# Selective-scan network in float32: B and C rows in one transfer per tile, layer 1's transfers on one queue, sums of pairs one unit later

## The chip, the cores and the metric

The kernel runs on one core of one Trainium2 chip. Its time is device microseconds of one execution, as the median of several. Everything is float32.

## The reference, cut to what matters

Four residual layers work on an image batch of 4 x 64 x 64 pixels with 192 channels, each on a group-normalised input. Layers 0 and 3 are two-dimensional selective scans (four directions over 4096 pixels), layer 1 is four Mamba blocks over the rows and columns (lines of 64 pixels, forwards and backwards), layer 2 is a Toeplitz layer. Nearly all the time goes into the selective scans:

```
def step(h, inp):                                   # over the pixels l
    u_l, dt_l, Bl, Cl = inp
    dA = exp(dt_l[..., None] * A)
    h  = dA * h + (dt_l * u_l)[..., None] * Bl[:, None, :]
    y  = sum(h * Cl[:, None, :], axis=-1)           # over 16 states
    return h, y
```

The channels are 384 in layers 0 and 1 and 192 in layer 3. B, C and dt come from a projection of u at every pixel; delta = softplus(projection of dt + bias).

## The kernel before, in words

**Units.** A job is one direction of one stretch of T = 512 pixels of one image; each of the three scan layers has 128 jobs. In a job, a unit (t, p, c) covers 64 channels (group g = 2t + c) and 4 of the 16 states (p of 4), as a tile of 128 partitions by 1024: 64 channels times two halves of the states on the partitions, two states times 512 pixels along each. A job of layers 0 and 1 has 24 units (three t of eight), one of layer 3 has 12. The order within a t is `TWO` (p, c): (0,0) (0,1) (3,0) (1,1) (1,0) (3,1) (2,0) (2,1), or `ONE`: p = 0, 3, 1, 2.

**What a unit does.** `feed` (two units ahead, AHEAD) writes b = dt * u * B into PSUM with 16 matmuls of dtuT against diagonal tiles (L374), and dA = exp(delta * A) with two activations on ScalarE (L397). `scan` runs the recurrence on VectorE into h (L407 in layer 1, two halves at L414 in layers 0 and 3, started from `carry`) and multiplies h by C on GpSimd (L418). `collect` sums the states with matmuls against `fold` into y (L443), always for two units together: pairs go onto the list `waiting` after each second unit, and one of two entries is taken in each unit that follows. For p = 3 ("direct": both groups in layers 1 and 3, c = 1 alone in layer 0) b comes from GpSimd instead: `spread` multiplies dtu2 by bc (L347), three units ahead (EARLY).

**Tiles and transfers.** B and C of a job are written from tile `xd` to DRAM (`bc_dram`, L226) and fetched back repeated over partitions: the tile `c` per p, and `bc` for p = 3 (L335). Each is filled by two transfers, one for each half of the partitions. `both` holds delta of one group, `dtu2` holds dt * u of one group, both twice over the halves. In layers 0 and 3 they are copied from SBUF (L317); in layer 1 from DRAM (`delta_dram`, `dtu_dram`, L322), with one transfer per tile, which is written

```
src = job["deltas" if name == "both" else "dtus"][key * 64 : (key + 1) * 64, :]
nc.sync.dma_start(one, src.unsqueeze(0).broadcast_to([2, 64, T]))
```

**What sets the order.** `run_jobs` writes the program unit by unit. Steps of a job (load, project, step sizes, turns, gating, outputs) stand at unit numbers relative to the job's first unit, in `when` and `steps`; what a step returns is done one unit later (`rest`). `plan` puts each fetch at the latest of: when its source is ready, LEAD = 12 units ahead of its first use, and when the tile that had its buffer was used last plus `behind`. Tiles come from pools with a number of buffers each (`bufs`); a transfer waits until its buffer is released. [...]nearly all transfers are issued by SyncE (SP), a few by ScalarE (ACT): bc_dram and delta_dram, and y in layers 0 and 3.

Layer 1's own steps are in `mamba_job`: `input_of` (convolution), `gate` (z), `gated` (u*D + y on VectorE, then times z on GpSimd) and `out`.

Of the kernel before, what the change touches and what calls it, by code (L numbers as in the profile page):

```python
# [7 lines left out]
F32 = mybir.dt.float32  # L8
# [8 lines left out]
N = 16  # L17
R = 12
E = R + 2 * N
T = 512  # L20
# [5 lines left out]
EARLY = 3  # L26
# [10 lines left out]
class Kernel:  # L37
# [66 lines left out]
    def run_jobs(self, jobs, pools):  # L104


        G = jobs[0]["DI"] // 64
        order = []
        for t in range(-(-G // 2)):
            order += [(t, *one) for one in (TWO if 2 * t + 1 < G else ONE)]  # L110
        units = [(k, *one) for k in range(len(jobs)) for one in order]
        per = len(order)
        steps = {}
        for k, job in enumerate(jobs):
            for at, step in self.prepare(job, pools) + job["steps"]:
                steps.setdefault(k * per + at, []).append(step)
        for at, load in self.plan(jobs, order, pools):
            steps.setdefault(at, []).append(load)
        start, end = min(steps), max(len(units) + 3, max(steps) + 1)
        waiting, rest = [], []  # L120
        for i in range(min(start, -EARLY), end + 4):
            if 0 <= i + AHEAD < len(units):
                k, t, p, c = units[i + AHEAD]
                self.feed(jobs[k], t, p, c, pools)
            todo = waiting[:1]
            if 0 <= i < len(units):
                k, t, p, c = units[i]
                after = self.scan(jobs[k], t, p, c, pools)
                if after is not None:
                    steps.setdefault(i + 1, []).insert(0, after)  # L130
            if 0 <= i + EARLY < len(units):
                k, t, p, c = units[i + EARLY]
                if c in jobs[k]["direct"].get(p, ()):
                    self.spread(jobs[k], t, p, c, pools)
            if 0 <= i < len(units):
                if (i + 1) % 2 == 0:
                    waiting += [(units[i][0], [one[1:] for one in units[i - 1 : i + 1]], n) for n in range(2)]


            if todo:  # L140
                k, two, n = waiting.pop(0)
                self.collect(jobs[k], two, n, pools)
                if n and two[1][1] == LAST:
                    steps.setdefault(i, []).append(lambda job=jobs[k], t=two[0][0]: job["add"](t))
            now, rest = rest + steps.pop(i, []), []
            for step in now:
                after = step()
                if after is not None:
                    rest.append(after)
        assert not rest and not steps and not waiting  # L150

    def plan(self, jobs, order, pools):


        uses, ready = {}, {}
        for k, job in enumerate(jobs):
            job["cbc"], job["bbc"], job["diag"], job["both"], job["dtu2"] = {}, {}, {}, {}, {}
            job["dtuT"] = {}
            when = {name: k * len(order) + at for name, at in job["when"].items() if isinstance(at, int)}

            near = 2 if job["carry"] is not None else 5
            dtu = when["finish"] + 3 if job["carry"] is not None else when["store"] + 5
            for j, (t, p, c) in enumerate(order):
                i, g = k * len(order) + j, 2 * t + c
                direct = c in job["direct"].get(p, ())
                reads = [("c", p, i, when["project"] + 6), ("both", g, i - AHEAD, when["finish"] + near)]
                if direct:
                    reads += [("bc", p, i - EARLY, when["project"] + 6), ("dtu2", g, i - EARLY, dtu)]
                else:
                    reads.append(("diag", p, i - AHEAD, when["turn_b"] + 5))  # L170
                for name, key, at, after in reads:
                    first, _ = uses.setdefault(name, {}).get((k, key), (at, at))
                    uses[name][k, key] = first, at
                    ready[name, k] = after
        loads = []
        for name, of in uses.items():
            bufs, turn = pools["bufs"][name], sorted(of, key=of.get)
            for j, (k, key) in enumerate(turn):
                first = of[k, key][0]
                at = max(ready[name, k], first - LEAD)  # L180
                if j >= bufs:
                    at = max(at, of[turn[j - bufs]][1] + pools["behind"])
                one = lambda part=None, job=jobs[k], name=name, key=key: self.fetch(job, name, key, pools, part)
                if name == "diag":


                    at = max(ready[name, k], first - (LEAD_DIAG if k else NB))
                    if j >= bufs:
                        at = max(at, of[turn[j - bufs]][1] + 3)
                    loads += [(first, at + part, lambda part=part, one=one: one(part)) for part in range(NB)]  # L190
                    at += NB - 1
                else:
                    loads.append((first, at, one))
                assert at < first, (name, k, key, at, first)
        return [one[1:] for one in sorted(loads, key=lambda one: one[0])]

    def prepare(self, job, pools):

        nc = self.nc
        prep, mm = pools["prep"], pools["mm"]  # L200
        P, NT, DI, w = job["P"], job["NT"], job["DI"], job["w"]
# [12 lines left out]
        def projected(ps):  # L214
            xd = job["xd"] = prep.tile([128, 256], F32, name="xd", bufs=1)
# [7 lines left out]
            else:  # L223
                by_half = job["bc"].rearrange("a (h l) -> h a l", h=2)
            for h in range(2):
                nc.scalar.dma_start(by_half[h], xd[h * 64 : h * 64 + 2 * N, :])  # L226
            job["delta"] = prep.tile([P, NT, T], F32, name="delta", bufs=1)
            job["dtu"] = prep.tile([P, NT, T], F32, name="dtu", bufs=1)
            if P < 128:
# [37 lines left out]
        def finish():  # L267
            delta = job["delta"]
            nc.scalar.activation(delta, delta, AF.Softplus)  # L269
            if job["carry"] is None:  # L270
                job["deltas"] = self.bcd.tile([DI, T], F32, name="delta_dram")
                nc.scalar.dma_start(job["deltas"].rearrange("(t p) l -> p t l", p=P), delta)

            def after():
                (nc.gpsimd if job["carry"] is None else nc.vector).tensor_mul(job["dtu"], delta, job["u"])  # L275

            return after

        def turn(t):
            ps = mm.tile([128, NB, P], F32, name="dtu_ps", tag="mm")  # L280
# [24 lines left out]
    def fetch(self, job, name, key, pools, part):  # L305
# [23 lines left out]
        else:  # L329
            one = pools[name].tile([128, 2 * T], F32, name=name)  # L330
            job["cbc" if name == "c" else "bbc"][key] = one
            for q in range(2):
                row = N + 8 * q + 2 * key if name == "c" else 4 * key + 2 * q
                src = job["bc"][row : row + 2, :].rearrange("a l -> (a l)")
                nc.sync.dma_start(one[q * 64 : (q + 1) * 64, :], src.unsqueeze(0).broadcast_to([64, 2 * T]))  # L335

    def spread(self, job, t, p, c, pools):

# [61 lines left out]
    def scan(self, job, t, p, c, pools):  # L400
# [1 line left out]
        rev, carry, g = job["rev"], job["carry"], 2 * t + c  # L402
        way = slice(None, None, -1) if rev else slice(None)
        b, dA, direct = job["fed"].pop((t, p, c))
        h = pools["work"].tile([128, 2 * T], F32, name="h", bufs=7 if carry is None else 3)
        if carry is None:
            nc.vector.tensor_tensor_scan(h[:, way], dA[:, way], b[:, way], 0.0, ALU.mult, ALU.add)  # L407
        else:
# [143 lines left out]
    def ss2d_scan(self, pre, u_d, y_d, P, NT, ways, A, dtb):  # L552
# [3 lines left out]
        with (  # L556
# [10 lines left out]
            tc.tile_pool(name="s_y", bufs=2, space=PSUM) as yp,  # L567
        ):
            pools = {"prep": prep, "work": work, "c": cp, "diag": dp, "both": both, "mm": mm, "b": bp, "y": yp,
                     "bc": bcp, "dtu2": dtu2, "bufs": bufs, "behind": 3}  # L570
            jobs = []
            carry = {
                (g, p): pw.tile([128, 2], F32, name=f"carry{g}_{p}", bufs=1)
                for g in range(DI // 64) for p in range(PAIRS)
            }
            when = {
                3: dict(load=-33, project=-29, turn_b=-27, step_size=(-21, -19, -17), finish=-15,
                        turn=(-13, -11, -9), direct={3: (1,)}),
                2: dict(load=-25, project=-21, turn_b=-19, step_size=(-17, -16), finish=-14,
                        turn=(-9, -8), direct={3: (0, 1)}),  # L580
            }[NT]
# [122 lines left out]
    def mamba(self, x_in):  # L704
# [6 lines left out]
        done = [[self.dram.tile([C, L], F32, name=f"m_out{i}_{b}") for b in range(B)] for i in range(2)]  # L711

        both_w = [self.dram.tile([P, NT, C], F32, name=f"m_both_w{i}") for i in range(4)]
        bufs = dict(c=4, bc=2, diag=4, both=4, dtu2=2)
        with (
            tc.tile_pool(name="n", bufs=2) as pn,
            tc.tile_pool(name="n_ps", bufs=2, space=PSUM) as psum,
# [27 lines left out]
        with (  # L745
# [12 lines left out]
            tc.tile_pool(name="m_y", bufs=2, space=PSUM) as yp,  # L758
        ):
            pools = {"prep": prep, "work": work, "c": cp, "diag": dp, "both": both, "mm": mm, "b": bp, "y": yp,  # L760
                     "bc": bcp, "dtu2": dtu2, "bufs": bufs, "behind": 2}
            fixed = [once.tile([P, 2 * T], F32, name=f"dA{j}") for j in range(3)]
            zero = once.tile([P, 2 * ROWS], F32, name="zero")
            nc.gpsimd.memset(zero, 0.0)
# [13 lines left out]
    def mamba_job(self, pw, pin, mm, i, begin, rev, w, x, done, both_w, c, fixed, zero):  # L778
# [69 lines left out]
        def gated(t):  # L848
# [3 lines left out]
                nc.vector.scalar_tensor_tensor(u, u, w["D"][:, t : t + 1], job["y"][t], ALU.mult, ALU.add)  # L852
                nc.gpsimd.tensor_mul(z, z, u)

            return after

        def parts(m):

# [30 lines left out]

            return after  # L890

        when = dict(project=-24, turn_b=-22, step_size=(-20, -19, -17), finish=-15, turn=(-9, -2, 3), store=-11)
        each = lambda f, ats: [(at, lambda t=t: f(t)) for t, at in enumerate(ats)]
        steps = [(-50, weights)] if begin else []
        steps += [(-46, load)] + each(input_of, (-37, -34, -31)) + each(gate, (-4, -1, 1)) + each(out, (30, 33))
        if rev:
            steps += each(earlier, (25, 28))
        job.update(
# [327 lines left out]
```

## Time and profile before

| | us |
|---|---|
| median of 3 runs | 31297.76 (31268.2 to 31301.49) |
| profiled execution | 31284.29 |
| its span | 31282.5 |
| scan of layer 0, each of four images | about 2278 (the first from 190.2 to 2468.4) |
| scan of layer 1 | 11188.7 (10806.8 to 21995.5) |
| scan of layer 3, each of four images | about 1264 to 1267 (the first from 25158.1 to 26421.8) |

The rest, some 5,700 us, is the inputs and outputs of layers 0 and 3, the norms and layer 2. The table by stretch gives, for every engine, the time in which it was busy; the share of the DMA engines is a mean over the core's 16. TensorE's busy time comes from modelled ends of matmuls, so that 90% is not its peak rate.

### The profile page before, as it was taken

How to read it: one execution, taken by the hardware profiler on the slowest of the kernel's cores; microseconds unless marked ns; L12 is line 12 of the kernel's file. 1: busy time of each engine (PE TensorE's matmuls, PEld its weight loads, DVE VectorE, ACT ScalarE, POOL GpSimd, SP SyncE). 2: the span in 40 equal slices, each digit the busy share in tenths (PEclk: the TensorE clock that was granted, in tenths of full speed). 3: DMA queues.
4: the chain of work that ended last, by engine and by line, in shares of the span. 5: the costliest groups of instructions: out<-in, count | busy, mean ns of one | idle time of the engine just before them, and what ended most of it. 6: DMA issues, size and time to landing. Idle time of an engine off the chain costs nothing. (4 is left out here: it accounts for less than half of the span.)

```text
span 31282.5 us, 503240 instructions
## 1 busy us (share of the span) xinstructions
PE 27353.4 (87%) x189464; PEld 16218.5 (52%) x189464; DVE 22344.0 (71%) x16587; ACT 23257.2 (74%) x50327; POOL 22884.2 (73%) x9831
## 2 busy tenths in 40 slices
PE   8998998998899699999889999998588988888888
PEld 5664654665466355555555555555355344444444
DVE  7887887888788677776667777676423277777777
ACT  7885885887688588887878888887232187878788
POOL 7885885888688499988889898888100077777777
PEclk9999999999999899999999999999799999999999
DMA  3333333333333433333333333333533344444444
GB/s 108 102 99 116 103 96 117 99 99 107 109 103 100 139 96 98 97 97 98 96 98 98 97 98 96 97 97 96 133 72 78 106 132 126 132 126 130 127 131 126
DMA packets 1606616, 3342.20 MB, mean 107 GB/s; under 512 B 350646, under 2 KB 407415, under 8 KB 1588567
## 3 DMA queue, kind: packets, MB, share of 16 engines
q1 hardware_dynamic: 1432150, 3033.08, 35.3%
q10 hardware_dynamic: 172032, 276.92, 2.6%
q8 instruction: 1497, 24.53, 0.3%
q14 instruction: 937, 7.67, 0.1%
HBM read 2149.81 MB, written 656.08 MB: 90 GB/s over the span
## 5 line engine op out<-in xcount | busy, mean ns | idle before, releaser
L374 PE MATMUL b<-diag,dtuT 128*64 128x256 f32 x98304 | 13308.4, 386 | 954.9 <-DVE h L414 759.4
L418 POOL TENSOR_TENSOR hc<-h,c 128x1024 f32<-128x1024 f32 x4608 | 10938.8, 2394 | 1641.9 <-DVE h L414 1336.6
L374 PEld LDWEIGHTS b<-diag,dtuT 128*64 128x64 f32 x98304 | 8544.2, 139 | 5362.7 <-issue 1770.1
L397 ACT ACTIVATE dA<-both,A 128x512 f32<-128x512 f32 (+1 forms) x12288 | 8308.5, 711 | 2062.3 <-DVE h L414 981.2
L414 DVE TENSOR_TENSOR_SCAN h<-dA,carry,b 128x512 f32<-128x512 f32 x6720 | 8180.2, 1263 | 1546.4 <-PE b L374 647.5
L418 POOL TENSOR_TENSOR h<-h,c 128x1024 f32<-128x1024 f32 x3072 | 7209.3, 2376 | 918.1 <-DVE h L407 570.0
L328 ACT ACTIVATE diag<-ident,bt 128x128 f32<-128x128 f32 x20480 | 6563.7, 391 | 106.9 <-issue 106.1
L407 DVE TENSOR_TENSOR_SCAN h<-dA,b 128x1024 f32<-128x1024 f32 x2304 | 5240.7, 2279 | 1701.4 <-PE b L374 829.2
L443 PE MATMUL y<-hc,fold 128*64 128x512 f32 x18432 | 5587.0, 605 | 534.0 <-POOL hc L418 533.3
L443 PE MATMUL y<-h,fold 128*64 128x512 f32 x12288 | 4736.9, 614 | 716.2 <-POOL h L418 713.0
L347 POOL TENSOR_TENSOR bs<-dtu,bc 128x1024 f32<-128x1024 f32 x1536 | 3642.2, 2371 | 452.8 <-issue 224.8
L497 POOL MEMSET pad<- 128x13068 f32 (+1 forms) x8 | 73.4, 9172 | 3974.3 <-DMA cw<-in_L_conv_w 3001.6
L443 PEld LDWEIGHTS y<-hc,fold 128*64 128x64 f32 x18432 | 1709.8, 139 | 1684.1 <-POOL hc L418 978.7
L397 ACT ACTIVATE b<-both,A 128x504 f32<-128x504 f32 (+1 forms) x3072 | 2074.0, 675 | 527.9 <-DVE h L414 438.3
L443 PEld LDWEIGHTS y<-h,fold 128*64 128x64 f32 x12288 | 1321.9, 139 | 1804.2 <-POOL h L418 1210.7
L407 DVE TENSOR_TENSOR_SCAN h<-b,bs 128x1024 f32<-128x1024 f32 x768 | 1752.7, 2282 | 650.8 <-ACT b L397 616.2
L414 DVE TENSOR_TENSOR_SCAN h<-b,carry,bs 128x512 f32<-128x512 f32 x1344 | 1638.8, 1260 | 111.8 <-ACT b L397 93.7
L235 PEld LDWEIGHTS dtu_ps<-ident,dtu 128*64 128x64 f32 (+1 forms) x16384 | 1165.4, 143 | 649.4 <-issue 307.6
L235 PE MATMUL dtu_ps<-ident,dtu 128*64 128x128 f32 (+1 forms) x16384 | 1309.6, 278 | 171.2 <-ACT z L839 125.3
L397 ACT ACT_TABLE_LOAD x1094 | 1403.6, 1283 | 15.2 <-DMA both<-delta_dram 2.6
L414 DVE TENSOR_TENSOR_SCAN h<-dA,b 128x512 f32<-128x512 f32 x960 | 1113.5, 1205 | 365.2 <-PE b L374 139.9
L275 DVE TENSOR_TENSOR dtu<-delta,u 128x1536 f32<-128x1536 f32 (+1 forms) x256 | 589.0, 2301 | 560.5 <-ACT delta L269 560.5
(157 smaller groups left out, 26136.2 us busy)
## 6 DMA issues: line engine op xcount, KB each, us to landing
c<-bc_dram SPq DMA_DIRECT2D x3072, 256.0 KB
both<-delta SPq DMA_DIRECT2D x2048, 128.0 KB
bc<-bc_dram SPq DMA_DIRECT2D x768, 256.0 KB
both<-delta_dram SPq DMA_DIRECT2D x768, 256.0 KB
dtu<-dtu_dram SPq DMA_DIRECT2D x768, 256.0 KB
dtu<-dtu SPq DMA_DIRECT2D x1280, 128.0 KB
L_y<-out ACTq DMA_DIRECT2D x512, 256.0 KB
u<-L_u SPq DMA_DIRECT2D x160, 768.0 KB
```

The lines of the kernel that those rows point to most:

```text
L235: nc.tensor.matmul(to[half * 64 : (half + 1) * 64], of[:, half * 64 : (half + 1) * 64], self.ident[:p, :p], start=True, stop=True,)
L275: (nc.gpsimd if job["carry"] is None else nc.vector).tensor_mul(job["dtu"], delta, job["u"])
L328: nc.scalar.activation(to, self.ident, AF.Copy, scale=of)
L347: self.nc.gpsimd.tensor_mul(by(b), dtu, by(job["bbc"][p]))
L374: nc.tensor.matmul(to, dtu, job["diag"][p][:, k, 2 * q : 2 * q + 2, :], start=True, stop=True,)
L397: nc.scalar.activation(to[n], of, AF.Exp, scale=w["A"][:, g, 2 * p + n : 2 * p + n + 1])
L407: nc.vector.tensor_tensor_scan(h[:, way], dA[:, way], b[:, way], 0.0, ALU.mult, ALU.add)
L414: nc.vector.tensor_tensor_scan(hn[:, n, way], dA[:, n, way], by_n[:, n, way], start, ALU.mult, ALU.add)
L418: nc.gpsimd.tensor_mul(hc, h, job["cbc"][p])
L443: nc.tensor.matmul(y[c * 64 : (c + 1) * 64, :], self.fold, of, start=first == 0 and n == 0, stop=last == LAST and n == 1)
L497: nc.gpsimd.memset(pad, 0.0)
```

## The change

- `fetch`: a `c` or `bc` tile is filled by one transfer for all 128 partitions, in all three scan layers; the source is a hand-written access pattern.
- `run_jobs`: in layer 1 (`lag` 1) a pair of units may be summed one unit later; in layers 0 and 3 (`lag` 0) as before.
- In layer 1 the stores to bc_dram and delta_dram are issued by SyncE; the latter stands one unit later.
- In layer 1 several steps stand at other units; `gated` returns its work one unit later; five c and three dtu2 buffers in place of four and two; `behind` is 3 in place of 2.
- In layers 0 and 3: four h buffers in place of three; in layer 0 the turns of dtu one unit later; the product dtu one unit later, with `near` and `dtu` to match.

```diff
 # run_jobs
-            todo = waiting[:1]
+            todo = waiting[:1] if waiting and waiting[0][0] <= i else []
...
                 if (i + 1) % 2 == 0:
-                    waiting += [(units[i][0], [one[1:] for one in units[i - 1 : i + 1]], n) for n in range(2)]
+                    two = [one[1:] for one in units[i - 1 : i + 1]]
+                    waiting += [(i + 1 + pools["lag"], units[i][0], two, n) for n in range(2)]
 # plan
-            near = 2 if job["carry"] is not None else 5
-            dtu = when["finish"] + 3 if job["carry"] is not None else when["store"] + 5
+            near = 3 if job["carry"] is not None else 5
+            dtu = when["finish"] + 4 if job["carry"] is not None else when["store"] + 5
 # prepare: projected
-                nc.scalar.dma_start(by_half[h], xd[h * 64 : h * 64 + 2 * N, :])
+                dma = nc.sync if job["carry"] is None else nc.scalar
+                dma.dma_start(by_half[h], xd[h * 64 : h * 64 + 2 * N, :])
 # prepare: finish
                 job["deltas"] = self.bcd.tile([DI, T], F32, name="delta_dram")
-                nc.scalar.dma_start(job["deltas"].rearrange("(t p) l -> p t l", p=P), delta)

             def after():
+                if job["carry"] is None:
+                    nc.sync.dma_start(job["deltas"].rearrange("(t p) l -> p t l", p=P), delta)
                 (nc.gpsimd if job["carry"] is None else nc.vector).tensor_mul(job["dtu"], delta, job["u"])

-            return after
+            return after if job["carry"] is None else lambda: after
 # fetch
-            for q in range(2):
-                row = N + 8 * q + 2 * key if name == "c" else 4 * key + 2 * q
-                src = job["bc"][row : row + 2, :].rearrange("a l -> (a l)")
-                nc.sync.dma_start(one[q * 64 : (q + 1) * 64, :], src.unsqueeze(0).broadcast_to([64, 2 * T]))
+            row, step = (N + 2 * key, 8) if name == "c" else (4 * key, 2)
+            of = job["bc"]
+            nc.sync.dma_start(one, bass.AP(of.tensor, of.offset + row * T, [[step * T, 2], [0, 64], [1, 2 * T]]))
 # scan
-        h = pools["work"].tile([128, 2 * T], F32, name="h", bufs=7 if carry is None else 3)
+        h = pools["work"].tile([128, 2 * T], F32, name="h", bufs=7 if carry is None else 4)
 # ss2d_scan, layer 0
-                        turn=(-13, -11, -9), direct={3: (1,)}),
+                        turn=(-12, -10, -8), direct={3: (1,)}),
 # mamba
-        bufs = dict(c=4, bc=2, diag=4, both=4, dtu2=2)
+        bufs = dict(c=5, bc=2, diag=4, both=4, dtu2=3)
...
-                     "bc": bcp, "dtu2": dtu2, "bufs": bufs, "behind": 2}
+                     "bc": bcp, "dtu2": dtu2, "bufs": bufs, "behind": 3, "lag": 1}
 # mamba_job: gated
-            return after
+            return lambda: after
 # mamba_job
-        when = dict(project=-24, turn_b=-22, step_size=(-20, -19, -17), finish=-15, turn=(-9, -2, 3), store=-11)
+        when = dict(project=-24, turn_b=-22, step_size=(-21, -19, -18), finish=-14, turn=(-9, -3, 8), store=-11)
-        steps += [(-46, load)] + each(input_of, (-37, -34, -31)) + each(gate, (-4, -1, 1)) + each(out, (30, 33))
+        steps += [(-46, load)] + each(input_of, (-36, -34, -31)) + each(gate, (-6, -4, -1)) + each(out, (33, 35))
```

More of the change, by code (lines that the diff above doesn't have):

```diff
@@ L120, in run_jobs @@
         waiting, rest = [], []
-        for i in range(min(start, -EARLY), end + 4):
+        for i in range(min(start, -EARLY), end + 6):
             if 0 <= i + AHEAD < len(units):
@@ L136, in run_jobs @@
                 if (i + 1) % 2 == 0:
-                    waiting += [(units[i][0], [one[1:] for one in units[i - 1 : i + 1]], n) for n in range(2)]
+                    two = [one[1:] for one in units[i - 1 : i + 1]]
+                    waiting += [(i + 1 + pools["lag"], units[i][0], two, n) for n in range(2)]
             if todo:
-                k, two, n = waiting.pop(0)
+                _, k, two, n = waiting.pop(0)
                 self.collect(jobs[k], two, n, pools)
@@ L569, in ss2d_scan @@
             pools = {"prep": prep, "work": work, "c": cp, "diag": dp, "both": both, "mm": mm, "b": bp, "y": yp,
-                     "bc": bcp, "dtu2": dtu2, "bufs": bufs, "behind": 3}
+                     "bc": bcp, "dtu2": dtu2, "bufs": bufs, "behind": 3, "lag": 0}
             jobs = []
```

## Prediction

> **What bounds the kernel now.** I read the page's first part, then the sums by stretch for the three scan stages, then the DMA view of short windows in which only one kind of transfer is on the wire. The page (busy us, share of the span, instructions):
>
> ```profile
> span 31282.5 us, 503240 instructions
> PE 27353.4 (87%) x189464; PEld 16218.5 (52%) x189464; DVE 22344.0 (71%) x16587; ACT 23257.2 (74%) x50327; POOL 22884.2 (73%) x9831
> ```
>
> No engine is full over the span, so the stages are read one by one: one image's scan in layer 0, all of layer 1's scan, one image's scan in layer 3 (start:end, length, busy us of PE, PEld, DVE, ACT, POOL, granted clock, DMA share, GB/s):
>
> ```profile
> 190.20:2468.40 2278.20, 2117.10 (x16610) 1370.47 (x16610) 1955.74 (x1612) 1899.48 (x4704) 2018.58 (x862) 0.97 0.37 98
> 10806.80:21995.50 11188.70, 10189.26 (x69944) 5865.09 (x69944) 7950.70 (x4715) 9341.64 (x17095) 9858.99 (x4359) 0.97 0.31 97
> 25158.10:26421.80 1263.70, 1102.30 (x8118) 661.78 (x8118) 992.56 (x828) 1172.50 (x2996) 1146.96 (x480) 0.99 0.49 131
> ```
>
> A layer-0 image is 32 jobs of 24 units: 2278.2/32 = 71.2 us a job. Layer 1 is 128 jobs of 24 units: 87.4 us. A layer-3 image is 32 jobs of 12 units: 39.5 us. TensorE (93%) and GpSimd (89%) bound layer 0, TensorE (91%) and GpSimd (88%) layer 1; in layer 3 TensorE, ScalarE and GpSimd are all near 90%. The DMA share looks harmless everywhere, 0.31 to 0.49, but it is a mean over 16 engines. Issues in all, and KB each:
>
> ```profile
> c<-bc_dram SPq DMA_DIRECT2D x3072, 256.0 KB
> bc<-bc_dram SPq DMA_DIRECT2D x768, 256.0 KB
> both<-delta_dram SPq DMA_DIRECT2D x768, 256.0 KB
> dtu<-dtu_dram SPq DMA_DIRECT2D x768, 256.0 KB
> ```
>
> Two windows take that mean apart. First, two c and two bc transfers (issued from 768.15 us on), nearly alone:
>
> ```profile
> DMA packets 320, 1.07 MB, mean 227 GB/s; under 512 B 63, under 2 KB 63, under 8 KB 319
> q1 hardware_dynamic: 319, 1.05, 89.6%
> ```
>
> 256 data packets of 4 KB in 4.7 us, all 16 engines busy, and 63 tiny packets: the four transfers' completion marks, about 16 each. Second, a window of 10.6 us in layer 1 (17917.3 to 17927.9) in which two both<-delta_dram transfers run, with SyncE's queue around it:
>
> ```profile
> DMA packets 250, 0.51 MB, mean 48 GB/s; under 512 B 2, under 2 KB 2, under 8 KB 250
> q1 hardware_dynamic: 250, 0.51, 12.6%
> 17915.32 1.16 SPq L322 DMA_DIRECT2D both<-delta_dram  x2
> 17920.93 0.48 SPq L322 DMA_DIRECT2D dtu<-dtu_dram  x1
> ```
>
> The same kind of transfer at 48 GB/s, on 12.6% of the engines: two of sixteen, with two marks. The two were issued within 1.2 us and run one after the other, **5.3 us each**: they share the same two engines, first come first served. So layer 1 already has a narrow place: both and dtu are 768/128 = 6 each a job, 12 x 5.3 = 63.6 of 87.4 us on two engines.
>
> [...]the source of both<-delta_dram is [2 copies][64 rows][512], [...]two marks; a c transfer is [64][1024], about 16 marks.[...]
>
> **The change part by part.**
>
> *B and C in one transfer (all three layers).* Removed: two transfers of [64][1024]. Added: one whose source is [2, step][64, step 0][1024] and whose target is 128 partitions. The outermost source size is 2, the form of both<-delta_dram, with packets of 4 KB in place of 2 KB. Price: twice 5.3 = **10.6 us on the two engines** (64 packets each), in place of two transfers at 4.7/4 = 1.2 us on sixteen. Bounds: 10.2 if a longer packet carries less overhead; 2.4 if the pattern is spread after all. Per job 4 c and 1 bc, 3072/2/384 and 768/2/384: 5 x 10.6 = 53.0 us. SyncE issues five transfers fewer a job (0.58 us each), which pays nothing, since it mostly waits.
>
> - Layer 1: 63.6 + 53.0 = 116.6 us a job on two engines. They also carry 1/16 of the rest: two 768 KB stores, 384 KB of xn, 384 KB out, half as often 384 KB in, some 160 KB per engine at 24 GB/s = 6.5 us. SyncE waits for the delta and dtu stores to land before it issues the next both, with little queued behind: about 3 us idle (it waited 78.2/64 = 1.2 us for one such store). Sum **126 us** against 87.4: +38.6 x 128 = **+4,940**. Ends: 118 (marks hidden, lower packet price) to 140 (idle gaps as below).
> - Layer 3: 53.0 + 6.5 (some 2.5 MB a job of both, dtu, u, out over 16) + 1.5 for gaps = **61 us** against 39.5: +21.5 x 128 = **+2,750**. Ends 55 and 68.
> - Layer 0: 53.0 + 11 (4.2 MB over 16) = 64 us, under 71.2, so no throughput limit, but a burst. Three c tiles can only be loaded once the last tasks of the job before have released theirs (units 17, 20, 21), and the last is read at unit 27: 10 units, 30 us. Before, they took 7 us; now 3 x 10.6 = 31.8 plus small transfers and landing, 33.5. GpSimd waits some 4 us, and the two bounding engines can make up part of it; I take **+4 us x 128 = +510**. Ends 0 (caught up) and +1,000.
>
> *Pairs summed a unit later (layer 1).* No instruction added; the y matmuls move one unit (3.6 us) back, past waits of TensorE for GpSimd: 1210.7 us (705 times) on weight loads and 713.0 us (485) on matmuls. What is late next is the gating of u by y. At best layer 1 falls to GpSimd's 9859 us, a gain of 1,330; at worst it costs some us a job where u is needed. Behind a queue of 126 us a job GpSimd has 40 us to spare, so I take **0**; the cover is the narrow pair of engines, and without it I would take half, -500 or so, with what follows.
>
> *All transfers by SyncE (layer 1).* Two bc_dram stores and one delta store a job leave ScalarE's queue, with ScalarE's wait for bc_dram (337.4 us, 54 times). On SyncE they stand in order between the loads: behind them queue the dtu, bc and both loads, and if ScalarE is late with delta all wait. Between -337 and +3 us a job; the gain is hidden like the last, the loss is in my 3 us of gaps.
>
> *Steps respaced, five c and three dtu2 buffers.* Instructions unchanged; loads start earlier. It smooths a queue but cannot add to the rate of two engines: 0, from -200 to +200.
>
> *Four h buffers, later dtu turns (layers 0 and 3).* VectorE waited 28.0 us an image for GpSimd in layer 0: at most -110 over four images. In layer 3 it is covered by the transfers. 0 is taken.
>
> Sum: 31,284 (the profiled execution, 31282.5 plus 1.8 around it; the shown median is 13 above, under 0.05%) + 4,940 + 2,750 + 510 = 39,484, about **39,480 us**.
>
> **The rivals.** *Spread over 16 engines (faster).* If the step of 4096 or 1024 in place of 0 in the outer dimension lets the transfer use 16 engines, nothing gets narrower and the waits above count: half of GpSimd's 1,330 idle us in layer 1, less some new lateness, about -550: 30,730 us. Against it: the order of sizes is that of both<-delta_dram, which ran on two. It decides from the first c transfer: 16 marks or 2. Chance 0.05, of which 0.01 within the noise.
>
> *Only layer 1 pays (slower, less).* Loads are asked for up to 12 units ahead, so layers 0 and 3 may hide them: 31,284 + 4,940 = 36,220. Against it: 53 us a job cannot hide under 39.5 in layer 3, whatever the lead. Chance 0.04.
>
> *The queue also stands idle (slower, more).* SyncE issues in order and waits for releases: 978.3 and 1527.7 us in layer 1 for GpSimd before line 322. If each wait now leaves the pair idle, with c tiles freed late and needed soon, layer 1 goes to 140, layer 3 to 68, layer 0 to +8 us: 31,284 + 6,730 + 3,650 + 1,020 = 42,700. For it: three c loads in one burst. Against: with compute ahead of its data the releases come early. Chance 0.16; the forecast keeps 0.75.
>
> **The numbers.** Lower ends together (118, 55, 0) give 37,190, upper ones 42,700; the range 36,900 to 42,300 leaves out the first two rivals and the worst of the third. Differences under 0.2% (63 us) count as none. Faster 0.04, same 0.01, slower 0.95.
>
> **What would show it.** Right: c transfers of 512 KB with two marks each at about 48 GB/s; GpSimd's scan products waiting for "DMA c<-bc_dram" (298.1 us over the whole run now) by thousands of us; all engines' shares down in layers 1 and 3, layer 0 nearly as before; layer 1's scan near 16.1 ms, layer 3's near 1.95 ms an image. Wrong: c transfers at over 200 GB/s, or layer 3 still at 39.5 us a job.

## The result, and the profile after

The changed kernel takes 40700.38 us (median of 4 runs, 40699.81 to 40713.34) against 31299.62 us for the kernel before beside it: a ratio of 1.3006, interval 1.2983 to 1.3028. That is 1,220 us above the forecast of 39,480 and inside its range. From the page of the profiled execution:

```profile
span 40697.9 us, 499183 instructions
PE 28508.9 (70%) x189464; PEld 16515.4 (41%) x189464; DVE 22385.6 (55%) x16587; ACT 23005.2 (57%) x50179; POOL 22906.4 (56%) x9831
DMA c<-bc_dram 16%; DMA both<-delta_dram 15%; PE b L376 8%; ACT diag L331 5%; ACT dA L399 5%; PE y L445 4%; DVE h L416 3%; POOL hc L420 2%; ACT L399 2%; ACT b L399 2%; DVE h L409 2%; SPq L325 2%; PE yt_ps L1078 1%; DMA xn<-t_xn 1%; PE conv_ps L531 1%
c<-bc_dram SPq DMA_DIRECT2D x1536, 512.0 KB
bc<-bc_dram SPq DMA_DIRECT2D x384, 512.0 KB
```

VectorE and GpSimd do what they did, to 50 us; their shares fall because the span grew. The third line is the chain that ended last, by line: transfers lead it, and its first two entries are the ones on a pair of engines: 12.6% of sixteen for both<-delta_dram in the prediction's second window, 13.1% for c in the view below. Half as many c and bc issues carry the same bytes. By stretch (columns as before): one image of layer 0, layer 1, one image of layer 3.

```profile
208.10:2869.00 2660.90, 2253.43 (x16610) 1573.71 (x16610) 1960.48 (x1612) 1899.24 (x4704) 2021.38 (x863) 0.91 0.28 84
12460.80:28239.30 15778.50, 10583.67 (x69942) 5309.36 (x69942) 7959.29 (x4715) 9104.49 (x16956) 9871.16 (x4359) 0.85 0.19 69
31431.50:33452.30 2020.80, 1148.32 (x8118) 672.11 (x8118) 996.89 (x828) 1168.72 (x2996) 1144.16 (x478) 0.81 0.26 82
```

Per job: layer 1 went from 87.4 to 123.3 us, layer 3 (mean of four images) from 39.5 to 63.5, layer 0 from 71.1 to 83.2. The mean DMA share fell in every stage, to 0.19 in layer 1, exactly where transfers became the bound: a mean over 16 engines does not see two. The DMA view of 17.4 us in layer 3 (32473.2 to 32490.6), in which c transfers are nearly alone, and SyncE's queue around it:

```profile
DMA packets 228, 0.91 MB, mean 52 GB/s; under 512 B 2, under 2 KB 2, under 8 KB 228
q1 hardware_dynamic: 228, 0.91, 13.1%
32449.24 0.54 SPq L337 DMA_DIRECT2D bc<-bc_dram  x1
32457.08 21.24 SPq L337 DMA_DIRECT2D c<-bc_dram  x4
32478.37 15.79 SPq L320 DMA_DIRECT2D both<-delta  x6
```

Two marks, 13.1% of sixteen engines, 52 GB/s: 226 packets of 4 KB on two engines in 17.4 us, 154 ns a packet and 9.9 us a tile. Marks are the packets under 512 B: in the prediction's second window two of them came between 17922 and 17923 us and two between 17927.5 and 17928.5, at the end of each transfer. The last two lines show something more. The column after the start runs from the beginning of a row's first issue to the end of its last, with waits for a free tile between them. The single issues follow (ns, shortest/median/longest): those two rows, then c in the layer-3 image after and before.

```profile
L337 SPq DMA_DIRECT2D c<-bc_dram x4: 482/1403/9789, 32457.1 to 32468.5; - x4
L320 SPq DMA_DIRECT2D both<-delta x6: 507/596/11509, 32478.4 to 32493.7; - x6
L337 SPq DMA_DIRECT2D c<-bc_dram x124: 482/551/12116, 31441.7 to 33415.3; - x124
L335 SPq DMA_DIRECT2D c<-bc_dram x248: 444/584/829, 25179.4 to 26384.2; - x124
```

Most issues still take some 0.55 us. But with a few long transfers outstanding one issue stood for 9.8 us and the next, of a small both transfer, for 11.5 us; in the kernel before no c issue of the image took over 0.83 us.

Who waited for whom, layer 1 first (total us, times, longest), then one image of layer 0:

```profile
ACT dA L399 <- DMA both<-delta_dram: 5315.1, 375, 31.2
POOL h L420 <- DMA c<-bc_dram: 2645.1, 128, 31.7
...
POOL hc L420 <- DMA c<-bc_dram: 237.9, 25, 11.9
```

In layer 1 the both tiles, whose transfers were not touched, are the ones most waited for: they share the pair with the c tiles. An experiment below takes them off it. In layer 0 one job looks like this, SyncE's queue first and then GpSimd, with its idle time and what ended it:

```profile
1016.11 0.55 SPq L337 DMA_DIRECT2D c<-bc_dram  x1
1025.08 2.88 SPq L337 DMA_DIRECT2D c<-bc_dram  x2
1052.92 4.66 POOL L420 TENSOR_TENSOR hc<-h,c 128x1024 f32<-128x1024 f32 x2 [7.37 <-DMA c<-bc_dram]
```

Three c loads are issued as tiles come free, and the product that needs the last of them starts 36.8 us after the first, 7.4 us after GpSimd was ready for it.

### The profile page after: what moved, and what is told of

Read it like the earlier page. It is cut to its first block, busy times and chain, and to the rows that moved or that the text cites. A ratio compares the mean times of both kernels' runs of the same rounds, so it can differ in the third digit from the quotient of the medians.

```text
span 40697.9 us, 499183 instructions
## 1 busy us (share of the span) xinstructions
PE 28508.9 (70%) x189464; PEld 16515.4 (41%) x189464; DVE 22385.6 (55%) x16587; ACT 23005.2 (57%) x50179; POOL 22906.4 (56%) x9831
## 4 chain that ended last, share of the span: by engine, by line
DMA 37%; PE 22%; ACT 21%; DVE 8%; issue 5%; POOL 4%; SPq 3%; ACTq 0%; POOLq 0%; DVEq 0%
DMA c<-bc_dram 16%; DMA both<-delta_dram 15%; PE b L376 8%; ACT diag L331 5%; ACT dA L399 5%; PE y L445 4%; DVE h L416 3%; POOL hc L420 2%; ACT L399 2%; ACT b L399 2%; DVE h L409 2%; SPq L325 2%; PE yt_ps L1078 1%; DMA xn<-t_xn 1%; PE conv_ps L531 1%
## 5 line engine op out<-in xcount | busy, mean ns | idle before, releaser
L376 PE MATMUL b<-diag,dtuT 128*64 128x256 f32 x98304 | 14287.1, 408 | 3766.7 <-DVE h L409 2610.0
L376 PEld LDWEIGHTS b<-diag,dtuT 128*64 128x64 f32 x98304 | 8876.0, 147 | 8540.2 <-DVE h L409 3240.1
L445 PE MATMUL y<-hc,fold 128*64 128x512 f32 x18432 | 6476.9, 618 | 1166.3 <-POOL hc L420 1162.7
L445 PE MATMUL y<-h,fold 128*64 128x512 f32 x12288 | 3786.4, 627 | 2420.2 <-POOL h L420 2420.2
L445 PEld LDWEIGHTS y<-hc,fold 128*64 128x64 f32 x18432 | 2080.6, 142 | 2408.0 <-POOL hc L420 1628.2
L445 PEld LDWEIGHTS y<-h,fold 128*64 128x64 f32 x12288 | 1061.1, 146 | 3438.6 <-POOL h L420 2538.9
L426 ACT COPY carry<-h 128x2 f32<-128x2 f32 x4608 | 821.0, 183 | 1795.7 <-DMA dtu<-dtu 1630.6
L825 DVE SCALAR_TENSOR_TENSOR u<-in_ps,conv_w,u 128x504 f32<-128x504 f32 (+2 forms) x1152 | 832.2, 723 | 1773.5 <-ACT u L820 1764.0
L292 ACT COPY dtuT<-dtu_ps 128x512 f32<-128x512 f32 (+1 forms) x1024 | 560.5, 547 | 2066.6 <-issue 1040.9
```

The costliest lines, as they stand in the source:

```text
L376: nc.tensor.matmul(to, dtu, job["diag"][p][:, k, 2 * q : 2 * q + 2, :], start=True, stop=True,)
L426: nc.scalar.copy(carry[g, p], hn[:, :, 0 if rev else T - 1])
L445: nc.tensor.matmul(y[c * 64 : (c + 1) * 64, :], self.fold, of, start=first == 0 and n == 0, stop=last == LAST and n == 1)
L825: nc.vector.scalar_tensor_tensor(u[:, :, to], ps[:, :, of], tap(3 - j), u[:, :, to], ALU.mult, ALU.add)
```

## The experiments

Each edit is against the changed kernel if nothing else is said; each ratio is to the kernel before, measured beside it. Stage lengths run from the start of the first product with C to the start of the last.

**Two halves again**

```diff
-            row, step = (N + 2 * key, 8) if name == "c" else (4 * key, 2)
-            of = job["bc"]
-            nc.sync.dma_start(one, bass.AP(of.tensor, of.offset + row * T, [[step * T, 2], [0, 64], [1, 2 * T]]))
+            for q in range(2):
+                row = N + 8 * q + 2 * key if name == "c" else 4 * key + 2 * q
+                src = job["bc"][row : row + 2, :].rearrange("a l -> (a l)")
+                nc.sync.dma_start(one[q * 64 : (q + 1) * 64, :], src.unsqueeze(0).broadcast_to([64, 2 * T]))
```

> The changed kernel with one part undone: each c or bc tile is filled by two transfers of 64 partitions again; everything else of the change stays. Theory (narrow pair: the whole loss comes from the merged transfer's outermost size of 2, which puts it on two DMA engines): the loss is gone and the waits taken out of layer 1 count, about 30,800 us (30,300 to 31,300), layer 1's scan 10,600 to 11,150 us. Rival (order: stores to bc_dram and delta_dram among the loads on SyncE, or the later sums, carry a part of the loss): over 31,800 us, with layer 1's scan over 11,700.

Measured: 30987.48 us, ratio 0.9898 (0.9883 to 0.9913). Layer 1 11,016 us, layer 3 1,231 an image, layer 0 2,279 as before. The merged transfer is the whole loss, and the rest of the change gains 312 us (1%): some 170 in layer 1 and 140 in layer 3. Layer 3 has two edits of its own, the fourth h buffer and the later product dtu; no run separates them.

**The merge alone, on the kernel before**

The same lines the other way round, in the kernel before.

> The kernel before with the merged transfer alone. Theory (narrow pair): the whole loss, 40,700 us give or take 600; layer 1 at 123 us a job, layer 3 at 63, layer 0 at 83. Rival (order): the loss needs the other parts too; then under 37,000 us.

Measured: 40611.28 us, ratio 1.2972 (1.2953 to 1.2992). The loss needs nothing else of the change. The whole change takes 89 us more, 0.2%, which is a sum of opposite parts in the two profiled executions: the rest of the change makes layer 1 some 120 us shorter (124.2 to 123.3 us a job), layer 0 some 140 longer (82.1 to 83.2) and layer 3 some 65 longer.

**One row for all 128 partitions**

```diff
-            nc.sync.dma_start(one, bass.AP(of.tensor, of.offset + row * T, [[step * T, 2], [0, 64], [1, 2 * T]]))
+            nc.sync.dma_start(one, bass.AP(of.tensor, of.offset + row * T, [[0, 128], [1, 2 * T]]))
```

> The changed kernel, but the source of the merged transfer is [128, step 0][1024] in place of [2, step][64, step 0][1024]: same bytes, one transfer, one number of issues, outermost size 128. The upper 64 partitions get the lower ones' rows of B and C, so half of the states use wrong coefficients. Theory (narrow pair): it runs on 16 engines, 2.4 us a tile, and the time is that of the kernel with two halves within 0.5%. Rival (size: a transfer of 512 KB to 128 partitions is itself slow, or fewer, larger transfers block the queue): near 40,000 us.

Measured: 30880.56 us, ratio 0.9865 (0.985 to 0.988). Same bytes, same number of issues, same size of a transfer: only the source pattern, with 128 in place of 2 outermost, differs, and 9,820 us go. A window of 2.1 us (29690.9 to 29693) with most of one c tile:

```profile
DMA packets 137, 0.50 MB, mean 236 GB/s; under 512 B 16, under 2 KB 16, under 8 KB 137
q1 hardware_dynamic: 137, 0.50, 64.2%
```

Sixteen marks now, where the changed kernel had two after 9.9 us. The time is 107 us (0.35%) below the kernel with two halves, nearly all of it in layer 1: merging by itself would help a little, if a pattern with the right rows spread as this one does.

**Both and dtu in halves too**

The two-halves kernel with, in layer 1:

```diff
-            nc.sync.dma_start(one, src.unsqueeze(0).broadcast_to([2, 64, T]))
+            for q in range(2):
+                nc.sync.dma_start(one[q * 64 : (q + 1) * 64, :], src)
```

> As the kernel with two halves, and in layer 1 each both and dtu tile is filled by two transfers of 64 rows in place of one whose source begins with [2, step 0]. Theory (narrow pair, which in the kernel before is busy 63.6 of 87.4 us a job with these): data of layer 1 lands 5 us a tile earlier, and layer 1 gains 1 to 3 us a job more, 100 to 400 us below the kernel with two halves. Rival (slack: TensorE and GpSimd bound layer 1 and the tiles are asked for early enough): the same within 0.2%; or slower by up to 200 us, by twelve more issues a job on SyncE.

Measured: 30874.79 us, ratio 0.9861 (0.9845 to 0.9878), 113 us below two halves alone; layer 1 10,902 us. So both and dtu on the pair, 63.6 us a job, cost a little even with the c tiles on sixteen engines; on the kernel before itself this was not run. This version is faster than both kernels.

**Layer 0 alone merged, with five and with seven c buffers**

```diff
+            if job["carry"] is not None and job["NT"] == 3:   # merged; two halves elsewhere
...
-        bufs = dict(c=5, bc=2, diag=5, both=6, dtu2=2) if NT == 3
+        bufs = dict(c=7, bc=2, diag=5, both=6, dtu2=2) if NT == 3   # the second of the two alone
```

> The changed kernel with the merged transfer in layer 0 alone; layers 1 and 3 fill c and bc with two transfers. Theory (narrow pair, and in layer 0 the burst of three c loads): layer 0's loss of the changed kernel comes alone, (2664 - 2279) x 4 = +1,540 us over the kernel with two halves and some 60 us more between the images, 32,550 us. Rival (the granted TensorE clock, or a state left by the other layers, makes layer 0 longer): under 31,900.

> As the kernel with the merged transfer in layer 0 alone, with seven c buffers in layer 0 in place of five, so that of a job's four c loads only the last waits for a tile of the job just ending. Theory (burst): the pair of engines has 64 of 71 us a job to do, so spread out it fits: layer 0 loses 0 to 5 us a job in place of 12, 31,000 to 31,650 us. Rival (rate: the queue's in-order service of the small both and dtu transfers behind 10.6 us each is what costs): as with five buffers, near 32,500.

Measured: 32623.03 us with five buffers (ratio 1.0427, 1.0411 to 1.0442), layer 0 at 2,668 us an image; 31567.34 us with seven (1.0091, 1.0075 to 1.0106), at 2,408. Of the 12 us a job that layer 0 lost, two more buffers take back 8. The wait of layer 0's product for c shows why, in the first image with five buffers:

```profile
POOL hc L426 <- DMA c<-bc_dram: 266.8, 29, 11.8
```

In the same stretch with seven buffers there is no such wait at all. The burst of loads that wait for tiles of the job before is the main part. The last 4 us a job stay open: small transfers behind the long ones, or ScalarE, which still stood 97.8 us an image before its `diag` line, where the profile names a c transfer that this line does not read.

**Four engines in place of two**

```diff
-            row, step = (N + 2 * key, 8) if name == "c" else (4 * key, 2)
-            of = job["bc"]
-            nc.sync.dma_start(one, bass.AP(of.tensor, of.offset + row * T, [[step * T, 2], [0, 64], [1, 2 * T]]))
+            for q in range(2):
+                row = N + 8 * q + 2 * key if name == "c" else 4 * key + 2 * q
+                of = job["bc"]
+                src = bass.AP(of.tensor, of.offset + row * T, [[0, 4], [0, 16], [1, 2 * T]])
+                nc.sync.dma_start(one[q * 64 : (q + 1) * 64, :], src)
```

> The changed kernel with each c or bc tile filled by two transfers of 64 partitions whose sources are written [4, step 0][16, step 0][1024]: the same packets, on four engines in place of two or sixteen. Theory (narrow pair): 2.65 us a transfer, 5 x 5.3 = 26.5 us a job on engines that in layer 1 also carry both and dtu: 63.6 + 26.5 + 9.5 = 99.6 us a job against 86 with two halves on sixteen, +1,700 us; in layers 0 and 3 it stays under the job's time and costs nearly nothing, up to 300 us together: about 32,850 us. Rival (any spread under 16 blocks the queue as two did): over 36,000. Rival (only the transfer's own latency counts, not the load on shared engines): within 300 us of the kernel with two halves.

Measured: 33300.38 us, ratio 1.0642 (1.0625 to 1.066). Layer 1 12,559 us, 98.1 us a job against 99.6 worked out. The DMA view of a stretch of layer 3 with c transfers (27714.7 to 27729.4):

```profile
q1 hardware_dynamic: 339, 1.31, 24.4%
```

A quarter of the engines (24.4% of sixteen), with a 4 outermost. Layer 0 lost 1 us a job, near what was expected; layer 3 lost 4.5, which was not, and makes the total 450 us longer than worked out. By the prediction's terms the four engines have some 35 us a job to do there (26.5, 6.5 and 1.5), under the 38.5 that a job takes; whether bursts or a term priced too low made the difference, no run shows.

**Merged c and bc, but both and dtu wide**

The changed kernel with the second diff of "both and dtu in halves too".

> The changed kernel with the merged c and bc transfers kept, and layer 1's both and dtu tiles filled by two transfers of 64 rows, which use 16 engines. Theory (load on the shared pair): layer 1's pair falls from 123 to 53 + 9.5 = 63 us a job, under 86; what stays is a burst as in layer 0, 0 to 12 us a job. Layer 1's scan 11,000 to 12,600 us in place of 15,776, in all 35,900 to 37,500 us. Rival (each c transfer's own 10.6 us is what layer 1 waits for): layer 1 over 14,000 us, in all over 38,900.

Measured: 35799.52 us, ratio 1.1443 (1.1426 to 1.146). Layer 1:

```profile
12456.50:23376.00 10919.50, 9720.32 (x69942) 5062.76 (x69942) 7955.70 (x4716) 9106.27 (x16957) 9857.67 (x4359) 1.00 0.30 99
```

With the merged c transfers unchanged layer 1 is 10,917 us, less than with two halves. (No view of this run shows the engines of the halves. Other transfers of 64 rows had sixteen marks each: in layer 0 of the kernel before two dtu<-dtu moved 128 packets of 2 KB with 32 marks, 1026 to 1032, and with both<-delta of that size 92.3% of sixteen engines were busy from 1084 to 1085.5.) ScalarE's wait for both, 5,315 us in the changed kernel, is gone from the profile, and GpSimd's for c fell from 2,645 us to 8.5. So it was not the length of the c transfer that layer 1 waited for, but the sum of what shared its two engines. I had allowed for a burst as in layer 0; no loss of that kind shows, and the time came out below the expected range. Layers 0 and 3, untouched here, kept their losses.

**Lag 0, and ScalarE's stores, on the two-halves kernel**

```diff
-                     "bc": bcp, "dtu2": dtu2, "bufs": bufs, "behind": 3, "lag": 1}
+                     "bc": bcp, "dtu2": dtu2, "bufs": bufs, "behind": 3, "lag": 0}   # the first alone
...
-                dma = nc.sync if job["carry"] is None else nc.scalar
-                dma.dma_start(by_half[h], xd[h * 64 : h * 64 + 2 * N, :])
+                nc.scalar.dma_start(by_half[h], xd[h * 64 : h * 64 + 2 * N, :])         # the second alone, and delta_dram too
```

> The kernel with two halves, with lag 0 in layer 1: pairs are summed as early as before, the rest of the change stays. Theory (the later sums free TensorE from waits for GpSimd): slower than the kernel with two halves by 100 to 600 us, all in layer 1's scan (11,016 us there). Rival (TensorE's waits move elsewhere): within 60 us.

> The kernel with two halves, with layer 1's stores to bc_dram and delta_dram issued by ScalarE as before, the latter in its old place. Theory (ScalarE's 337 us of waits for bc_dram are worth something): slower than the kernel with two halves by 50 to 330 us. Rival (they are off the path): within 60 us.

Measured: lag 0 30999.38 us (ratio 0.9904, 0.9891 to 0.9918), 12 us from the kernel with lag 1, within 0.2%. Stores by ScalarE 31175.22 us (0.9958, 0.9945 to 0.9972), 188 slower, with layer 1 at 11,203 us where the kernel before has 11,186. So with the rest of the change in place the move to SyncE is worth all that layer 1 gained, and the later sums show nothing. How the move gains is not shown: with the stores back on ScalarE its wait for bc_dram is 99.8 us, where it was 337 in the kernel before, and the stage lost 187. Layer 1 of the two-halves kernel with lag 1, then with lag 0:

```profile
PEld b L377 <- DVE h L410: 1872.7, 1361, 8.4
PEld y L446 <- POOL h L421: 49.5, 45, 13.3
...
PEld b L377 <- DVE h L410: 1405.5, 999, 6.2
PEld y L446 <- POOL h L421: 475.1, 342, 11.9
```

The wait of the y matmuls for GpSimd went from 475 to 50 us, and the wait of the b matmuls for VectorE grew by 467: TensorE waits as long, one instruction later.

## Why the prediction was right, and where its terms were off

- *The narrow pair.* Right: two marks, 13.1% of sixteen engines. The step from the outermost size to the number of engines was taken from two forms in the kernel before (2 in front: 12.6%; 64: 89.6%), and the runs follow it: 24.4% with 4 in front, 64.2% and sixteen marks with 128. The price was 10.6 us a tile, twice that of a both tile with its 2 KB packets; it ran at 9.9, below the lower bound of 10.2: a packet of 4 KB took 154 ns, one of 2 KB some 85 (10.6 us on two engines for 248).
- *Layer 1: +4,940.* It was +4,590, 123.3 us a job for 126: five tiles at 9.9 in place of 10.6 us make up 3.5 us. The sum of loads is confirmed from both sides, by both and dtu made wide (10,917 us) and by four engines (98.1 us a job). The sign I had named, GpSimd waiting for c, came (2,645 us); the longest wait, ScalarE's for both, I had not named.
- *Layer 3: +2,750.* It was +3,068, 63.5 us for 61, though the tile was cheaper than priced. The term that was too low is the other transfers. A DMA share of 0.26 of sixteen engines in 2020.8 us is some 263 us of engine time a job; without the 99 us of c and bc, and spread evenly, that leaves an estimated 10 us on each engine, for my 6.5. With five tiles at 9.9 us it makes some 60; the remaining 4 us would be gaps, for my 1.5. SyncE's stalled issues were not in the sum. Layer 1 came out 350 us under its forecast and layer 3 318 over it; that they nearly cancel is luck. The 1,220 us by which the total was missed are layer 0's 1,039 and what lies outside the stages.
- *Layer 0: +510, with an end at +1,000.* **This step failed: +1,549, 12 us a job.** I had the burst and its place, but priced its wait at 4 us and let the two bounding engines make up part of it. In the job shown above the three loads took 36.8 us, where I had 33.5, and GpSimd was ready after 29.4. On average it waited 237.9/32 = 7.4 us a job, and the stage lost more than that, so nothing was made up. Seven buffers show the burst to be 8 of the 12 us; the merge alone, without the later dtu turns and the fourth h buffer, loses 11 of the 12. TensorE's granted clock in layer 0 fell from 0.97 to 0.91 meanwhile; no run separates what that cost.
- *Outside the stages.* Not in the sum: some 210 us of starts and gaps (some 5,920 us before, not 5,700 as I wrote, and some 6,130 after). The likely reason, not tested, is that a stage's first c tiles are loaded with nothing to hide them. From the last product of the first image to the first of the second: 364 us before, 385 after.
- *Edits taken at 0 under cover.* Right as a sum: the merge alone costs as much as the whole change. The parts were not 0, but some 120 us won in layer 1 and 210 lost in layers 0 and 3. For the case without cover I wrote that half of GpSimd's idle time in layer 1 would go, some 500 us, with the later sums and what follows them. It was 170 us, and the later sums gave 12 of it, not clear of the spread of the runs: VectorE's scan was the next wait. The move to SyncE, which I had between -337 us in all and +3 us a job, is -188. The fourth h buffer in layers 0 and 3 I took at 0; there, with the later product dtu, layer 3 gained some 35 us an image without the merged transfer, layer 0 nothing.
- *The rivals.* The spread over 16 engines was worked out at 30,730 us; one row for all gives 30,881. That is near in part by luck: I expected 550 us less in layer 1 alone, and it was 270 there and 137 in layer 3. That only layer 1 pays fell with layers 0 and 3. The idle queue stood at 140, 68 and +8 us a job for layers 1, 3 and 0; it was 123.3, 63.5 and +12, so it fits layer 0 at most, and layer 1 ran below the forecast.

## What to carry to other kernels

Before two transfers are merged into one, look at the outermost size of the source pattern. With the same packets of 4 KB, 2 and 4 in front gave two and four engines here (13.1% and 24.4% of sixteen), 64 and 128 gave sixteen (89.6%, and 64.2% in a window with sixteen marks; the tiles filled had 64 or 128 partitions in front), so the broadcast of two halves written with the 2 in front got two. Add up the time of all transfers that land on those engines per job and compare it with the job, since the mean DMA share hides a full pair at 0.19 to 0.26. And a wait that is long in the profile is worth removing only if the engine is not held up at once by the next one.

## What the runs showed of the hardware that I had not expected

The time of an issue changed with what was queued: behind four long c transfers the first of six small both issues took SyncE 11.5 us, while the other five took 0.5 to 0.7, and in the kernel before six took 3.7 us together. In layer 1 of the kernel before, whose both and dtu were on two engines already, an issue of c took up to 9.2 us; with both and dtu wide none took over 0.55, though c was on the pair. So small transfers paid for long ones although most engines were idle: in the 11.5 us of that first both issue (32478.4 to 32489.9) 12.7% of sixteen were busy.

TensorE's granted clock was lower in the stages in which the changed kernel left TensorE idle: 0.81 in place of 0.99 in a layer-3 image (busy 57% of it in place of 87%), 0.85 in place of 0.97 in layer 1 (67% in place of 91%), and 1.00 in layer 1 when both and dtu were wide (89%). TensorE's longest wait in layer 1 of the changed kernel was 30.1 us (a weight load of b for VectorE's h). What sets the clock, no run shows. TensorE was busy 10,584 us in layer 1 against 10,189 with the same matmuls; no run shows how much of that is the clock's.
